# Two small edits in a graph network on one core: the row scaling with one VectorE operation fewer, and a split of rows issued earlier in the first pass

## The chip, the core and the metric

The kernel runs on one core of one Trainium2 chip. The metric is the device time of one execution, in microseconds (us). The engines are called PE (TensorE, matmuls), PEld (its weight loads), DVE (VectorE), ACT (ScalarE), POOL (GpSimd) and SP (SyncE, which here only issues DMAs). Each engine takes its instructions in the order written, and waits where an input or a buffer isn't ready.

## The reference, cut to what matters

Two layers are computed on 16 graphs of 1024 nodes and 128 channels. The first is a gated graph network (four rounds, with a layer norm), which takes up the first 1290 us and isn't touched. The second thins out each adjacency matrix (`adj_d`) and runs three SAGE passes over it, each with a batch norm; then comes a linear head and a layer norm.

```python
def _sage(x, adj, Wr, Wx, b, mf):
    deg = jnp.clip(jnp.sum(adj, axis=-1, keepdims=True), 1.0, None)
    agg = jnp.einsum('bij,bjd->bid', adj, x) / deg
    out = agg @ Wr + x @ Wx + b
    nrm = jnp.maximum(jnp.linalg.norm(out, axis=-1, keepdims=True), NORM_EPS)   # NORM_EPS = 1e-12
    return out / nrm * mf[..., None]

h1 = _bn(jax.nn.relu(_sage(x,  adj_d, Wr1, Wx1, b1, mf)), g1, be1)
h2 = _bn(jax.nn.relu(_sage(h1, adj_d, Wr2, Wx2, b2, mf)), g2, be2)
h3 = _bn(jax.nn.relu(_sage(h2, adj_d, Wr3, Wx3, b3, mf)), g3, be3)
```

The change is in the last line of `_sage`: each row is divided by its norm, which is kept from below 1e-12, and multiplied by the node's mask.

## The kernel before, in words

After the gated layer and the thinning, the class `Sage` runs the passes one after the other. A graph's 1024 rows lie in 8 tiles of 128 partitions, and are worked on in two halves of 4 tiles (512 rows), `f` = 0 and 1. In every pass and for every half, the steps from the matmul results to the finished rows are these:

- `scale_rows` (L1409 to L1419): the aggregated rows times the reciprocal degree (L1417 on DVE; in the third pass L1415 on ACT), plus the second matmul result (L1418 on DVE), gives `s_o`.
- `squares` (L1421 to L1427) on ACT: four sums of squares and a square root give `s_ss`, the norms, one for each row: 128 partitions x 4. The third pass shares them between ACT and DVE (`shared_squares`, L1429).
- `rows` (L1444 to L1452) on DVE: maximum with 1e-12 (L1446), reciprocal (L1447), times the mask (L1448), all on 128x4; then the rows with relu, times these factors (L1451), give `s_r`. In the third pass `rows_by_pool` (L1454) does the same three small operations on DVE (L1456 to L1458), and POOL does the scaling (L1461). There are 66 calls of `rows` (32 each in passes one and two, 2 in pass three) and 30 of `rows_by_pool`.

The first two passes also aggregate the new rows over the adjacency matrix for the pass after. For that the rows are kept as a high and a low part in the matmul's rounded type: `split` (L1464) copies them to `p_rh` on ACT (L1466), and POOL subtracts to get `p_rl` (L1467). `p_at` is the thinned adjacency matrix, transposed.

**The first pass** is a loop over units, one for each graph b, with 16 slots each (`slot`, L1657). No scheduler reorders anything: all engines are under a manual schedule, and the order in `slot` is that of each engine's queue. While graph b is aggregated and its rows are finished, the matrix of graph n = b + 1 is made ready in the same slots:

- `unit` (L1529): four matmuls turn a part of the removal pattern into `p_u`, then ACT writes part of the mask `p_at` from it (L1542). `p_u` has two buffers. In slot 8 ACT writes the whole of it, 128x512.
- `unit_low` (L1545): DVE writes the rest of the mask (L1550). In slot 8 there is none.
- `pack` (L1553): POOL casts the `p_at` of the slot before to bytes (`p_b`, L1558). In slot 8 it packs that of slot 7. SP stores the finished half in slot 10 (L1755).

For graph b, in this order: slots 0, 1, 3, 4 aggregate x (L1618); slots 5 and 7 do `out_first` for the two halves (L1627: `p_oa` and `p_ob`); slots 6 and 8 `scale_rows` and, later in the slot, `squares`; slots 7 and 9 `rows` for half 0 and half 1; slots 8 and 10 `split_r` for half 0 and half 1; slots 11 and 13 transpose the rows (L1472). Slots 9, 10, 12, 14 are the second product (L1618 again): 8 matmuls each, with `p_rh` of half 0, `p_rl` of half 0, `p_rh` of half 1, `p_rl` of half 1. Slots 7 and 12 also split the next graph's x into `p_xh` and `p_xl` on ACT and POOL, and in some slots DVE tests an input tile (L2107).

So the order in slot 8 is: the mask step of the next graph (`unit`), the packing (`pack`), `scale_rows` of half 1, `split_r` of half 0, `squares` of half 1, and a transposition of the next x.

**The second pass** (`slot_second`, L1852) has 8 slots for a graph and the same `rows` in slots 2 and 4. **The third** (`third`, L1917) goes through 32 halves with a distance of two between `scale_rows` and `rows_by_pool`, and ends in the head (`last`).

Of the kernel before, what the change touches and what calls it, by code (L numbers as in the profile page):

```python
# [15 lines left out]
ALU = mybir.AluOpType  # L16
# [349 lines left out]
class Norm:  # L366
# [5 lines left out]
    def __call__(self, out, rows):  # L372
        nc = self.nc
        st = self.pool.tile([P, NB, 6], F32, name="ln_st")
        mv = self.pool.tile([P, NB, 2], F32, name="ln_mv")
        for k in range(NB):
            nc.vector.bn_stats(st[:, k, :], rows[:, k, :])
        for k in range(NB):
            nc.vector.bn_aggr(mv[:, k, :], st[:, k, :])
        rs = self.pool.tile([P, NB], F32, name="ln_rs")  # L380
        nc.scalar.activation(rs, mv[:, :, 1], AF.Sqrt, bias=self.eps)
        nc.vector.reciprocal(rs, rs)
        for k in range(NB):
            nc.vector.tensor_scalar(out[:, k, :], rows[:, k, :], mv[:, k, 0:1], rs[:, k:k + 1],
                                    op0=ALU.subtract, op1=ALU.mult)


def sage_layers(ctx, tc, cst, adj, mask, not_r, summed, x1, W, vec, Wl, bl, out):
# [37 lines left out]
    def transposed(src, n, evac):  # L426
# [6 lines left out]
        return dst  # L433

    def sage(l, b, rows, ht, at, rd, mf, stats, psa, pso):

        pa = [psa.tile([C, HF], F32, name=f"s_a{f}") for f in range(2)]
# [57 lines left out]
    with ExitStack() as c1:  # L495
# [7 lines left out]
        for b in range(B):  # L503
# [36 lines left out]
            for f in range(2):  # L540
                nc.sync.dma_start(adj_t[b][4 * f:4 * f + 4].rearrange("k p n -> p k n"), at4[f])
            mf = row_tile("s_mf", mask[b])
            sage(0, b, rows, ht, at, rd, mf, stats, psa, pso)
        affine = batch_norm(0, stats)

# [85 lines left out]
class FixPoint:  # L631
# [206 lines left out]
    class Block:  # L838
# [22 lines left out]
        def rows(self, g):  # L861
            fix, nc = self.fix, self.fix.nc
            w = fix.wide.tile([P, N], BF, name="f_w", bufs=2)
            nc.vector.tensor_scalar(w, self.us[g], self.q[:, 2, g:g + 1], 0.5, op0=ALU.not_equal, op1=ALU.subtract)
            nr = fix.wide.tile([P, N], BF, name="f_nr", bufs=5)
            nc.vector.tensor_mul(nr, w, self.a[g])
            nc.sync.dma_start(fix.not_r[self.b0 + g, self.k * P:(self.k + 1) * P, :], nr)
            fix.read_last(self.i, g, nr)
# [49 lines left out]
class Gated:  # L918
# [25 lines left out]
    def bank(self):  # L944
        return self.ps6.tile([P, HF], F32, name="h_g")
# [264 lines left out]
class Sage:  # L1210
# [232 lines left out]

    def rows(self, b, f, o, ss):  # L1444
        nc = self.nc
        nc.vector.tensor_scalar(ss, ss, 1e-12, None, op0=ALU.max)  # L1446
        nc.vector.reciprocal(ss, ss)  # L1447
        nc.vector.tensor_mul(ss, ss, self.cst["mask"][:, 4 * f:4 * f + 4, b])  # L1448
        r = self.wk.tile([P, 4, C], F32, name="s_r")
        sc = ss.rearrange("p (k o) -> p k o", o=1).to_broadcast([P, 4, C])  # L1450
        nc.vector.scalar_tensor_tensor(r, o, 0.0, sc, op0=ALU.max, op1=ALU.mult)  # L1451
        return r  # L1452

    def rows_by_pool(self, b, f, o, ss):  # L1454
        nc = self.nc
        nc.vector.tensor_scalar(ss, ss, 1e-12, None, op0=ALU.max)  # L1456
        nc.vector.reciprocal(ss, ss)
        nc.vector.tensor_mul(ss, ss, self.cst["mask"][:, 4 * f:4 * f + 4, b])  # L1458
        r = self.wk.tile([P, 4, C], F32, name="s_r")
        for i in range(4):  # L1460
            nc.gpsimd.tensor_scalar(r[:, i, :], o[:, i, :], ss[:, i:i + 1], 0.0, op0=ALU.mult, op1=ALU.max)  # L1461
        return r
# [194 lines left out]
    def slot(self, b, t):  # L1657

        nc, g, n = self.nc, self.g.get(b), b + 1
        now, nxt = b >= 0, n < B  # L1660

        if nxt:
            if t in (4, 6):
                self.load_nr(n + 1, (t - 4) // 2)
            if t == 7:
                self.load_s(n + 1)
            if t == 10:
                self.load_a(n, 2)
            if t == 13 and n == B - 1:
                self.load_a(n, 3)  # L1670
        loads = {2: 3, 5: 4, 8: 5}
        if b == 0:
            loads = {0: 6, 1: 7, **loads}
        if b == B - 1:
            loads = {0: 4, 2: 5, 4: 7}
        if now and t in loads:
            self.load_a(b, loads[t])

        if now:
            if t in (2, 5):  # L1680
                g["ag", t // 5] = self.evict(g.pop(("pa", t // 5)), -1, 0)
            if t == 15:
                g["ag2"] = [self.evict(g.pop(("pb", f)), b, f) for f in range(2)]
        if nxt:
            self.unit(n, t)
            if t != 6 or not now:
                self.unit_low(n, t)
            if t:
                self.pack(n, t - 1)
        if now and t == 0:  # L1690
            self.pack(b, 15)
        if now:
            bank = lambda: self.ps3.tile([C, HF], F32, name="p_ag")
            if t in (2, 5):
                self.degrees(b, t // 5)
            if t in (0, 1, 3, 4):
                f, lo = t // 3, t in (1, 4)
                if not lo:
                    g["pa", f] = bank()
                self.agg(g["pa", f], (self.xh, self.xl)[lo], g["at"], f, range(NB), not lo, lo)  # L1700
            if t in (5, 7):
                self.out_first(b, t // 7)
            if t in (6, 8):
                f = t // 8
                g["o", f] = self.scale_rows(b, f, g.pop(("oa", f)), g.pop(("ob", f)))
                if t == 6 and nxt:
                    self.unit_low(n, t)
            if t in (3, 6):
                pt = bank() if t == 6 else self.ps1.tile([P, 4, P], F32, name="s_tr").rearrange("p a b -> p (a b)")
                self.degree_columns(b, t // 6, pt[:, :4])  # L1710
            if t in (7, 9):
                f = t // 9
                g["r", f] = self.rows(b, f, g.pop(("o", f)), g.pop(("ss", f)))
            if t in (8, 10):
                self.split_r(b, t // 10)
            if t in (6, 8):
                g["ss", t // 8] = self.squares(g["o", t // 8])
            if t in (11, 13):
                self.turn_r(0, b, t // 13, self.ps1)
            if t in (9, 10, 12, 14):  # L1720
                part = g["rl"] if t in (10, 14) else g["rh"]
                js = range(4 * (t // 12), 4 * (t // 12) + 4)
                for f in range(2):
                    if t == 9:
                        g["pb", f] = bank()
                    self.agg(g["pb", f], part, g["at"], f, js, t == 9, t == 14)

        if nxt:
            if t < 2:
                self.norm_stats(n, t)  # L1730
            if t in (2, 3):
                self.norm(n, t - 2)
            if t in (6, 8):
                self.turn_x(n, t // 8)
            if t in (7, 12):
                self.split_x(n, t // 12)
        tests = {2: 2, 10: 3, 12: 4, 14: 5}
        if b == 0:
            tests = {5: 6, 8: 7, **tests}
        if b == B - 1:  # L1740
            tests = {2: 2, 4: 3, 6: 4, 8: 5, 10: 7}
        if now and t in tests:
            self.check(b, tests[t])

        if now:
            if t == 2:
                nc.sync.dma_start(self.at8[b, 1], g["b", 1])
            if t == 7:
                for i in range(3):
                    nc.sync.dma_start(self.rho[b, i:i + 1, :], g["rho"])  # L1750
            if t in (13, 15):
                nc.sync.dma_start(self.rt[b, t // 15], g["rt", t // 15])
        if nxt:
            if t == 10:
                nc.sync.dma_start(self.at8[n, 0], self.g[n]["b", 0])  # L1755
            if t == 13:
                nc.sync.dma_start(self.x1[n], self.g[n]["s"])
        if (b, t) == (-1, 11):
            self.load_given()
        if (b, t) == (-1, 15):  # L1760

            for i in range(3):
                nc.sync.dma_start(self.rho[:, 3 + i, :], self.mask48[:B, :])
        if (b, t) == (0, 3):
            self.first_weights()
        if t == 1 and b >= 1:
            for f in range(2):
                nc.sync.dma_start(self.ag[b - 1, f], self.g[b - 1]["ag2"][f])
            del self.g[b - 1]
# [426 lines left out]
```

## Time and profile before

| | |
|---|---|
| median of 3 runs | 2141.18 us (2138.12 to 2145.97) |
| the profiled execution | 2138.47 us, its span 2136.5 us |
| PE busy | 2052.7 us, 96% of the span |
| DVE, POOL, ACT busy | 1814.3 (85%), 1333.8 (62%), 1305.9 (61%) |
| first pass, graph by graph | about 1291 to 1713 us of the span, 25.92 us for a unit in the middle |
| second pass | about 1714 to 1958 us |
| third pass | about 1958 to 2066 us, then the head |

In the rows of the profile, `out<-in` are the names of the tiles, and the two numbers ahead of an instruction in the timeline are its start and its duration in us. What stands in square brackets is the time for which the engine was idle before it, and what released it. Ends of matmuls are modelled, as they overlap.

### The profile page before, as it was taken

How to read it: one execution, taken by the hardware profiler on the slowest of the kernel's cores; microseconds unless marked ns; L12 is line 12 of the kernel's file. 1: busy time of each engine (PE TensorE's matmuls, PEld its weight loads, DVE VectorE, ACT ScalarE, POOL GpSimd, SP SyncE). 2: the span in 40 equal slices, each digit the busy share in tenths (PEclk: the TensorE clock that was granted, in tenths of full speed). 3: DMA queues.
4: the chain of work that ended last, by engine and by line, in shares of the span. 5: the costliest groups of instructions: out<-in, count | busy, mean ns of one | idle time of the engine just before them, and what ended most of it. 6: DMA issues, size and time to landing. Idle time of an engine off the chain costs nothing. (4 is left out here: it accounts for less than half of the span.)

```text
span 2136.5 us, 33076 instructions
## 1 busy us (share of the span) xinstructions
PE 2052.7 (96%) x10219; PEld 1435.3 (67%) x10219; DVE 1814.3 (85%) x4194; ACT 1305.9 (61%) x3127; POOL 1333.8 (62%) x1451
## 2 busy tenths in 40 slices
PE   7999999999999999999999988999999989999987
PEld 4566556665566666556665646888888768888876
DVE  4898998988998889998889997888888778887887
ACT  3657557566566565665656656666666545555756
POOL 5458558557467467566476446766677545665866
PEclk9999999999999999999999998999999999999999
DMA  8348346348436357456276346777777489996515
GB/s 252 88 105 252 88 128 224 79 119 240 103 102 222 88 168 188 93 167 184 69 212 159 89 147 245 287 289 286 288 290 285 170 294 341 339 336 222 157 45 161
DMA packets 233855, 406.15 MB, mean 190 GB/s; under 512 B 79042, under 2 KB 100196, under 8 KB 233668
## 3 DMA queue, kind: packets, MB, share of 16 engines
q1 hardware_dynamic: 189348, 284.64, 40.2%
q0 software_dynamic: 41616, 117.98, 20.6%
q8 instruction: 83, 1.36, 0.3%
q10 hardware_dynamic: 2704, 1.31, 0.2%
q14 instruction: 104, 0.85, 0.1%
HBM read 313.48 MB, written 109.25 MB: 198 GB/s over the span
## 5 line engine op out<-in xcount | busy, mean ns | idle before, releaser
L1104 PE MATMUL h_g<-h_h,h_wh 128*128 128x512 f32 x768 | 396.2, 597 | 4.0 <-DVE h_r L1116 4.0
L1104 PE MATMUL h_g<-h_ms,h_wi 128*128 128x512 f32 x768 | 392.2, 592 | 0.0
L1123 POOL TENSOR_TENSOR h_zh<-h_r,h_h 128x512 f32<-128x512 f32 x126 | 174.7, 1387 | 256.4 <-ACT h_r L1119 253.1
L737 DVE TENSOR_TENSOR_SCAN f_rank<-f_a,f_first,f_pd 128x1024 f16<-128x1024 bf16 x128 | 299.4, 2345 | 4.2
L1092 PE MATMUL h_g<-h_a,h_hi 128*128 128x512 f32 x1024 | 278.7, 413 | 1.1 <-DMA h_a<-in_adj_dram 1.0
L1104 PEld LDWEIGHTS h_g<-h_ms,h_wi 128*128 128x128 f32 x768 | 145.5, 190 | 184.3 <-issue 167.9
L1092 PE MATMUL h_g<-h_a,h_lo 128*128 128x512 f32 x1024 | 261.8, 392 | 0.1
L1558 POOL CAST p_b<-p_at 128x512 uint8<-128x512 f32 x256 | 203.7, 817 | 86.9 <-DVE p_at L1550 48.5
L1092 PEld LDWEIGHTS h_g<-h_a,h_hi 128*128 128x128 f32 x1024 | 190.1, 188 | 61.9 <-issue 20.8
L1092 PEld LDWEIGHTS h_g<-h_a,h_lo 128*128 128x128 f32 x1024 | 189.8, 188 | 38.7 <-DVE h_lo L1030 0.6
L1104 PEld LDWEIGHTS h_g<-h_h,h_wh 128*128 128x128 f32 x768 | 133.3, 190 | 101.2 <-issue 72.6
L1125 POOL TENSOR_TENSOR h_h<-h_h,h_zh 128x512 f32<-128x512 f32 x126 | 179.8, 1427 | 9.9
L1119 ACT ACTIVATE h_r<-h_r,h_bi 128x512 f32<-128x512 f32 x128 | 92.4, 722 | 150.7 <-DVE h_r L1118 150.7
L1124 POOL TENSOR_TENSOR h_zh<-h_z,h_zh 128x512 f32<-128x512 f32 x126 | 162.2, 1287 | 9.9
L1095 ACT COPY h_ms<-h_g 128x512 f32<-128x512 f32 x128 | 73.8, 577 | 150.0 <-PE h_g L1092 149.7
L1425 ACT ACTIVATE s_junk<-s_o 128x128 bf16<-128x128 f32 x256 | 76.1, 298 | 130.3 <-DVE s_o L1418 130.3
L910 ACT ACTIVATE f_u<-f_rank,f_q 128x128 f16<-128x128 f16 (+7 forms) x128 | 110.5, 866 | 70.6 <-DVE f_rank L850 69.6
L2107 DVE SCALAR_TENSOR_TENSOR p_a<-p_a 128x1024 bf16<-128x1024 f32 x96 | 126.3, 1315 | 0.0
L778 POOL TENSOR_SCALAR_AFFINE_SELECT f_both<-f_both 128x512 bf16<-128x512 bf16 x32 | 20.6, 642 | 163.9 <-DVE f_both L777 163.9
L1838 PE MATMUL q_ob<-s_wxp,q_xt 128*128 128x256 f32 x512 | 122.3, 382 | 0.0
L887 ACT ACTIVATE f_pd<-f_rank,f_q 128x128 f32<-128x128 f16 x128 | 59.1, 462 | 98.0 <-DVE f_q L701 94.8
L1550 DVE SCALAR_TENSOR_TENSOR p_at<-p_nr,p_u 128x128 fp32r<-128x128 bf16 (+1 forms) x192 | 102.6, 541 | 16.5 <-ACT p_at L1542 10.0
(306 smaller groups left out, 4895.8 us busy)
## 6 DMA issues: line engine op xcount, KB each, us to landing
h_a<-in_adj_dram POOLq DMA_DIRECT2D x128, 512.0 KB, 9.3
p_a<-in_adj_dram SPq DMA_DIRECT2D x96, 512.0 KB
f_a<-in_adj_dram POOLq DMA_DIRECT2D x128, 256.0 KB, 6.4
e_nr<-f_nr SPq DMA_DIRECT2D x128, 256.0 KB
p_nr<-e_nr SPq DMA_DIRECT2D x32, 1024.0 KB
s_at<-p_b SPq DMA_DIRECT2D x32, 512.0 KB
s_ag<-s_ag SPq DMA_DIRECT2D x64, 256.0 KB
q_agi<-s_ag SPq DMA_DIRECT2D x32, 512.0 KB
```

The costliest lines, as they stand in the source:

```text
L737: nc.vector.tensor_tensor_scan(out, a, other[:, 0, 0:1].to_broadcast([P, N]), start, op0=ALU.add, op1=ALU.bypass)
L910: nc.scalar.activation(u[:, :n1], rank[:, g, :n1], AF.Abs, bias=q[:, 1, g:g + 1], scale=q[:, 0, g:g + 1])
L1092: nc.tensor.matmul(pm[f], part[:, j, :], st.adj[j][:, half[f]], start=(j == 0 and n == 0), stop=(j == NB - 1 and n == 1))
L1104: nc.tensor.matmul(pg, lhs, rhs, start=(i == 0), stop=(i == len(mm) - 1))
L1119: nc.scalar.activation(r, r, AF.Tanh, bias=bias(self.bi, 2))
L1123: aid.tensor_tensor(d, r, h, ALU.subtract)
L1124: aid.tensor_tensor(d, z, d, ALU.mult)
L1125: aid.tensor_tensor(h, h, d, ALU.add)
L1550: self.nc.vector.scalar_tensor_tensor(g["at"][:, j, c0:c0 + low], v[:, j, c0:c0 + low], 0.0, pu[:, :low], op0=ALU.is_lt, op1=ALU.is_lt)
L1558: self.nc.gpsimd.tensor_copy(g["b", f][:, j, :], g["at"][:, j, f * HF:(f + 1) * HF].bitcast(F32))
L1838: nc.tensor.matmul(pb[:, i], g["xt"][:, f, blk], self.wxp, start=(i % 2 == 0), stop=False)
L2107: nc.vector.scalar_tensor_tensor(junk, a, 0.0, a, op0=ALU.is_gt, op1=ALU.not_equal, accum_out=bad[:, c:c + 1])
```

## The change

In `rows` and `rows_by_pool` the maximum ahead of the reciprocal is taken out. The reciprocal is taken of the norm itself, and the mask's multiplication becomes one operation that first takes the minimum with 1e12. In `slot`, `split_r` of half 0 moves from behind `scale_rows` in slot 8 to ahead of `unit` and `pack`. `split_r` of half 1 in slot 10 stays.

```diff
     def rows(self, b, f, o, ss):
         nc = self.nc
-        nc.vector.tensor_scalar(ss, ss, 1e-12, None, op0=ALU.max)
         nc.vector.reciprocal(ss, ss)
-        nc.vector.tensor_mul(ss, ss, self.cst["mask"][:, 4 * f:4 * f + 4, b])
+        nc.vector.scalar_tensor_tensor(ss, ss, 1e12, self.cst["mask"][:, 4 * f:4 * f + 4, b],
+                                       op0=ALU.min, op1=ALU.mult)
         r = self.wk.tile([P, 4, C], F32, name="s_r")
...
     def rows_by_pool(self, b, f, o, ss):
         nc = self.nc
-        nc.vector.tensor_scalar(ss, ss, 1e-12, None, op0=ALU.max)
         nc.vector.reciprocal(ss, ss)
-        nc.vector.tensor_mul(ss, ss, self.cst["mask"][:, 4 * f:4 * f + 4, b])
+        nc.vector.scalar_tensor_tensor(ss, ss, 1e12, self.cst["mask"][:, 4 * f:4 * f + 4, b],
+                                       op0=ALU.min, op1=ALU.mult)
...
     def slot(self, b, t):
...
             if t == 15:
                 g["ag2"] = [self.evict(g.pop(("pb", f)), b, f) for f in range(2)]
+            if t == 8:
+                self.split_r(b, 0)
         if nxt:
             self.unit(n, t)
...
-            if t in (8, 10):
-                self.split_r(b, t // 10)
+            if t == 10:
+                self.split_r(b, 1)
```

## The prediction

> **What bounds the kernel now.** I read the page first, for the engine that has no slack, then PE's waits, then a table by stage, and last the order in time of one unit of the first pass, where the moved step lies.
>
> ```profile
> span 2136.5 us, 33076 instructions
> ...
> PE 2052.7 (96%) x10219; PEld 1435.3 (67%) x10219; DVE 1814.3 (85%) x4194; ACT 1305.9 (61%) x3127; POOL 1333.8 (62%) x1451
> ...
> PE 33%; DVE 3%; ACT 2%; POOL 1%; issue 1%; DMA 0%; DVEq 0%; ACTq 0%; POOLq 0%
> ```
>
> PE is busy 96% of the span and has far the largest share of the chain that ended last. A shorter DVE step is worth something only where PE, or that chain, stands waiting for it. So the next view is PE's waits over the whole span; columns are total us, times, longest.
>
> ```profile
> PE p_ag L1618 <- ACT p_rh L1466: 10.2, 16, 2.2
> ...
> PE s_tr L1472 <- DVE s_r L1451: 3.3, 3, 1.7
> ...
> PE p_ag L1618 <- POOL p_rl L1467: 0.9, 1, 0.9
> ```
>
> The first is the largest of all of PE's waits: once in each of the 16 units of pass one, PE stands until ScalarE has written the high part `p_rh` of the first half's rows. The timeline gives 0.64 us to unit 0 and 2.20 to unit 15 (which has no next unit beside it), so 10.2 - 0.64 - 2.20 = 7.4 is left for 14 units, 0.52 each. The table by stage, over 13 of these:
>
> ```profile
> core 0: us, PE busy (x) PEld busy (x) DVE busy (x) ACT busy (x) POOL busy (x), PEclk, DMA share, GB/s
> 1341.50:1679.00 337.50, 330.16 (x2498) 271.76 (x2497) 281.67 (x756) 233.32 (x664) 236.96 (x261) 1.00 0.77 279
> ```
>
> 337.5 - 330.2 = 7.3 us of PE idle: nearly all of it is this wait. A unit lasts 25.92 us (the second product starts at 1419.81 and again at 1445.74). No other engine is over 84% here. Now the last steps before the wait, in one unit:
>
> ```profile
> 1417.33 0.20 ACT L1426 ACTIVATE s_ss<-s_ss 128x4 f32<-128x4 f32 x1
> ...
> 1417.57 0.17 DVE L1446 TENSOR_SCALAR s_ss<-s_ss 128x4 f32<-128x4 f32 x1
> 1417.78 0.18 DVE L1447 RECIPROCAL s_ss<-s_ss 128x4 f32<-128x4 f32 x1
> ...
> 1417.99 0.17 DVE L1448 TENSOR_TENSOR s_ss<-s_ss,mask 128x4 f32<-128x4 f32 x1
> ...
> 1418.26 0.69 DVE L1451 SCALAR_TENSOR_TENSOR s_r<-s_o,s_ss 128x512 f32<-128x512 f32 x1
> ...
> 1418.66 0.60 ACT L1542 ACTIVATE p_at<-p_u 128x512 fp32r<-128x512 f32 x1
> ...
> 1418.90 0.39 PE L1537 MATMUL p_u<-ident_b,p_nr 128*128 128x128 bf16 x4
> 1419.15 0.61 ACT L1466 CAST p_rh<-s_r 128x512 fp32r<-128x512 f32 x1
> ...
> 1419.81 2.11 PE L1618 MATMUL p_ag<-p_at,p_rh 128*128 128x512 f32 x8 [0.52 <-ACT p_rh L1466]
> ```
>
> The rows `s_r` are done at 1418.95, but `p_rh` starts at 1419.15: ScalarE's mask step of slot 8 (L1542) came first. PE's own work is done at 1419.29 and it starts 0.52 later. The same unit goes on, with the second half of the rows:
>
> ```profile
> 1420.60 1.29 POOL L1467 TENSOR_TENSOR p_rl<-s_r,p_rh 128x512 fp32r<-128x512 f32 x1
> ...
> 1421.84 0.60 POOL L1558 CAST p_b<-p_at 128x512 uint8<-128x512 f32 x1
> 1421.93 0.54 DVE L1446 TENSOR_SCALAR s_ss<-s_ss 128x4 f32<-128x4 f32 x1 [1.59 <-ACT s_ss L1426]
> ...
> 1421.97 2.09 PE L1618 MATMUL p_ag<-p_at,p_rl 128*128 128x512 f32 x8
> ...
> 1424.13 0.62 ACT L1466 CAST p_rh<-s_r 128x512 fp32r<-128x512 f32 x1 [0.77 <-DVE s_r L1451]
> ...
> 1424.80 2.12 PE L1618 MATMUL p_ag<-p_at,p_rh 128*128 128x512 f32 x8
> ```
>
> Two deadlines lie right behind the wait: the low part `p_rl` ends at 1421.89 and PE wants it at 1421.97; the second half's `p_rh` ends at 1424.75 and PE starts on it at 1424.80. Neither shows as a wait, neither has slack. If PE comes earlier, they must come earlier too.
>
> **What the Trainium skill says.** "VectorE: DVE Perf Modes", section "Rules for kernel authors": on DVE the number of operations counts. The trace agrees for four elements a row: 147 to 178 ns of busy time, 200 to 210 ns from start to start. "SBUF — State Buffer", section "Who interferes with whom": a DVE operation with two SBUF inputs can't run beside a GpSimd one that reads SBUF, nor can a `tensor_scalar` in a two-port mode; the later waits for the whole of the earlier. The trace agrees: L1446 lasts 169 ns in the median, but 540 above, until POOL's cast ended at 1422.44, and 929 at worst; L1451 goes from 694 to 1752.
>
> **Part 1, one DVE operation fewer (96 calls).** Out go a TENSOR_SCALAR (0.15 to 0.17 us) and a TENSOR_TENSOR (0.165), in comes one SCALAR_TENSOR_TENSOR on 128x4. The trace has it on 128x8 (L1581, 0.17 us); I take 0.17. Bounds: 0.15, and 0.93 when POOL holds the port (L1446's worst). Net: one start-to-start step, 0.20 us less from `s_ss` to `s_r`. Where it counts:
> - First pass, first half: it is on the chain to PE's wait. Second half: 0.20 us inherited, because DVE takes up the second half's scaling (L1417, L1418) right behind `s_r`, and 0.20 of its own or more, as the operation that goes is the one POOL held up.
> - Second pass: nothing in the steady part. PE is busy 213.7 of 217 us between 1728 and 1945, and that hides it. At its start (1726 to 1731) the chain runs through L1446 twice and PE waits for `s_r`: 2 x 0.20 = 0.4 us. The blocked L1451 at 1731.32 (1.75 us, behind POOL's low part) could give more (0.9) if DVE now gets there first, or only 0.2.
> - Third pass: PE is the bound (96.7 of 98 us). One dip (1975 to 1990) has L1456 on the chain: 0.2 us (0 to 0.5). At the end the last two `rows` stand in DVE's queue on the chain (2061.91 and 2063.89): 2 x 0.20 = 0.4.
>
> **Part 2, the split of half 0 moved up.** It issues two instructions and no DMA: ScalarE's copy to `p_rh` (0.61), now ahead of the mask step L1542 of slot 8, and POOL's subtraction to `p_rl` (1.29), now ahead of the packing of slot 7 (0.60). ScalarE: `p_rh` follows `s_r` at once, 1418.95 - 0.20 = 1418.75, start 1418.80 instead of 1419.15. Gain **0.35 us**, of which 0.20 is part 1 and 0.15 the order. PE would start at 1419.46; its own work ends at 1419.29, so 0.17 us of the wait is left. Behind `p_rh` now queues L1542, done about 1419.9 instead of 1419.26; its readers are the packing of slot 8 and, by its buffer, the mask matmuls of slot 10 (1421.77), and the squares behind it begin at 1420.2: covered. POOL: `p_rl` starts when the low part of x ends (1420.0) instead of behind a packing (1420.60), and ends at about 1421.3. PE wants it at 1421.97 - 0.35 = 1421.62. Without this the gain would be lost here, as 1421.89 is too late. The packing of slot 7 ends at 1421.9 instead of 1420.63; SP's store of the packed half waits for it (issued 1420.65, now about 1421.9), and behind it SP has nothing until 1425.75: no cost.
> Second half: `s_ss` 1421.50 to 1421.70, reciprocal 1421.73, the new operation 1421.94 but held by a packing to about 1422.4, `s_r` 1422.67 to 1423.36 (1423.9 if held too), `p_rh` done at 1424.0 (1424.6). PE wants it at 1424.80 - 0.05 - 0.35 = 1424.40. It fits, or costs 0.2.
>
> **Sum.** Units 1 to 14: 14 x 0.35 = 4.9. Unit 0: 0.2 at `p_rh`, then PE's 0.9 us wait for `p_rl`, of which 0.1 to 0.9 goes (POOL and the input test L2107 start within 0.1 us of each other there): 0.6. Unit 15: no masks to pass, 0.2. Start of the second pass 0.4, dip 0.2, end 0.4. Together **6.7 us**. The profiled execution took 2138.47 (span 2136.5 and 2.0 around it), so 2131.8; the median of the three runs is 2.7 above it, and from that 2141.2 - 6.7 = **2134.5 us**.
>
> **Rivals.**
> - *The wait goes wholly, and the locks fall well* (0.20): 7.4 in units 1 to 14, 1.1 in unit 0, 0.2, 0.9, 0.5 and 0.4: 10.5, so 2130.7. For it: the 0.17 us left rests on modelled matmul ends. Against: the chain has only 0.35 to give.
> - *The wait moves to slot 12* (0.14): the second `p_rh` comes only at 1424.6, PE loses 0.2 again, 14 x 0.15 + 1.8 = 3.9, so 2137.3. For it: zero slack before. Against: that half gains 0.4 by itself.
> - *Slower: POOL's shifted packings hold the second half's DVE steps* (0.08). Three casts and `p_rl` now run nearly without a gap from 1420.0 to 1422.5, where the new two-input operation and `s_r` fall. With the worst durations seen (0.93 and 1.75), `s_r` ends at 1424.7 and PE starts at 1425.4, 0.6 later than now: 14 x 0.6 = 8.4, less the other 1.8: +6.6, so 2147.8. It decides against the change once `s_r` of the second half ends later than it did, 1424.1. Against: POOL is free after 1422.5 until the next `p_rh`.
> - *The change doesn't do what it says*: where the new operation is as slow as the two it replaces, only the order counts, 14 x 0.15: inside the second rival's range.
>
> **Chances.** The main case has 0.58. A measurement tells about 0.5% from no change, 10.7 us. Faster by more: about 0.6 of the first rival and 0.08 of the main case (run-to-run spread here is 8 us), 0.17. Slower by more: some half of the slower rival and a rest for the unseen, 0.06. Within: 0.77. The range reaches from gains of 12.5 to a loss of 2.3: 2128.7 to 2143.5.
>
> **What will show it.** Right: DVE has 96 instructions fewer; the wait of L1618 for `p_rh` falls from 0.52 to about 0.17 in a unit and its total to some 5 us; a unit lasts 25.57; `p_rh` of half 0 stands ahead of slot 8's L1542, `p_rl` ahead of the packing. Wrong: a new wait of PE for `p_rl` in slot 10 or `p_rh` in slot 12, L1451 longer in the second half, or a unit that stays at 25.92.

## The result, and the profile after

The median went from 2141.83 us (7 runs) to **2131.95 us** (7 runs): a ratio of **0.9963, with a 95% interval of 0.9952 to 0.9974**, that is 7.9 us less (5.6 to 10.3). The ratio on record isn't the quotient of the two medians: these lie 9.9 us apart (0.9954), which is inside the interval too. A second measurement of the changed kernel on another occasion gave 0.9964 (0.9951 to 0.9977). The profiled execution took 2132.37 us. Its page begins:

```profile
span 2130.4 us, 32979 instructions
...
PE 2052.9 (96%) x10218; PEld 1437.5 (67%) x10219; DVE 1784.6 (84%) x4098; ACT 1304.9 (61%) x3127; POOL 1339.8 (63%) x1451
```

DVE has 4194 - 4098 = 96 operations fewer; PE is as busy as it was, so what went is waiting. PE's waits in the changed kernel (us, times, longest):

```profile
PE p_ag L1618 <- ACT p_rh L1466: 5.5, 16, 2.0
...
PE q_ag L1878 <- POOL q_at L1829: 3.4, 2, 1.9
...
PE s_tr L1472 <- DVE s_r L1451: 1.1, 2, 0.7
```

The wait that the change aims at fell from 10.2 to 5.5 us. In the second pass the wait for `s_r` fell too, but one for POOL's unpacking (`q_at`) stands in its place, once at the start of the pass (1.86 us) and once at its end (1.56). And the same unit of the first pass as the prediction shows, in the timeline of the changed kernel:

```profile
1416.90 0.17 DVE L1447 SCALAR_TENSOR_TENSOR s_ss<-s_ss,mask 128x4 f32<-128x4 f32 x1
...
1417.17 0.69 DVE L1451 SCALAR_TENSOR_TENSOR s_r<-s_o,s_ss 128x512 f32<-128x512 f32 x1
...
1417.95 0.62 ACT L1466 CAST p_rh<-s_r 128x512 fp32r<-128x512 f32 x1 [0.30 <-DVE s_r L1451]
...
1418.47 0.59 ACT L1542 ACTIVATE p_at<-p_u 128x512 fp32r<-128x512 f32 x1
...
1418.62 2.12 PE L1618 MATMUL p_ag<-p_at,p_rh 128*128 128x512 f32 x8 [0.22 <-ACT p_rh L1466]
1418.95 1.31 POOL L1467 TENSOR_TENSOR p_rl<-s_r,p_rh 128x512 fp32r<-128x512 f32 x1
...
1420.79 2.09 PE L1618 MATMUL p_ag<-p_at,p_rl 128*128 128x512 f32 x8
...
1420.84 0.18 DVE L1446 RECIPROCAL s_ss<-s_ss 128x4 f32<-128x4 f32 x1 [1.58 <-ACT s_ss L1426]
1421.05 0.33 DVE L1447 SCALAR_TENSOR_TENSOR s_ss<-s_ss,mask 128x4 f32<-128x4 f32 x1
...
1422.21 0.62 ACT L1466 CAST p_rh<-s_r 128x512 fp32r<-128x512 f32 x1
```

The copy to `p_rh` now goes ahead of the mask step, and ScalarE waits 0.30 us for `s_r` where before it was busy. PE's wait is 0.22 instead of 0.52. `p_rl` is done at 1420.26, half a microsecond ahead of PE (1420.79); the second half's `p_rh` at 1422.83, 0.76 ahead of PE (1423.59).

Where the time went, from the starts of PE's matmuls in the two traces (us):

| stretch | before | after | difference |
|---|---|---|---|
| start to the first aggregation of unit 0 (not touched) | 1293.1 | 1294.4 | +1.3 |
| from there to the second product of unit 1 | 48.9 | 47.5 | -1.4 |
| 13 units more | 337.0 | 332.5 | -4.4 |
| from unit 14's second product to the first matmul of pass two (`q_oa`) | 39.9 | 37.9 | -2.0 |
| pass two: to the second graph's first matmul | 19.5 | 21.0 | +1.6 |
| rest of pass two | 215.0 | 215.1 | +0.1 |
| pass three, to the head's bank start (L1405) | 118.4 | 116.6 | -1.8 |
| head | 64.8 | 65.3 | +0.6 |

A unit lasts (1674.39 - 1341.88)/13 = 25.58 us instead of 25.92. Only the row of the 13 units is as steady as that: in the two traces of the changed kernel a unit agrees within 0.01 us. Other rows also move where nothing was edited. In the second trace of the changed kernel (k8), for instance, the second row is 46.0 and not 47.5 us, and with the first pass as before (k6) it is 50.3 and not 48.9. Over all traces the start took 1291.2 to 1294.4 us and the head 64.8 to 66.7, in no order that follows the edits. The experiments show what of the other rows belongs to the change.

### The profile page after: what moved, and what is told of

It reads as the page before. It is cut to its first block, busy times and chain, and to the rows that moved or that the text cites. A ratio compares the mean times of both kernels' runs of the same rounds, so it can differ in the third digit from the quotient of the medians.

```text
span 2130.4 us, 32979 instructions
## 1 busy us (share of the span) xinstructions
PE 2052.9 (96%) x10218; PEld 1437.5 (67%) x10219; DVE 1784.6 (84%) x4098; ACT 1304.9 (61%) x3127; POOL 1339.8 (63%) x1451
```

## Experiments

Each has a short name (k1 to k9), by which later sections refer to it. Ratios are to the kernel before. A diff is against the changed kernel unless the text says otherwise.

**Each part alone.** First part 1 without the move (k1):

```diff
-            if t == 8:
-                self.split_r(b, 0)
...
-            if t == 10:
-                self.split_r(b, 1)
+            if t in (8, 10):
+                self.split_r(b, t // 10)
```

> Part 1 alone: the DVE operation fewer in rows and rows_by_pool, the split of half 0 left behind the mask step and the packing. Theory (two gates): in units 1 to 14 the copy to p_rh waits for whichever comes last, s_r or ScalarE's mask step, and that step can't begin before PE's p_u of slot 8; the copy would start 0.49 us behind it as before. So the unit stays at 25.92 us and the wait at 0.52, though s_r is 0.20 us earlier; what is left is unit 15 and the third pass, 0.5 to 2 us of the whole. Rival (the two parts add up, 0.20 and 0.15, as the prediction's sum had it): the unit is 25.72, the wait 0.32, and the whole 3.5 to 5 us shorter than before.

Ratio to before 0.9991 (0.9983 to 1.0000). A unit lasts (1680.87 - 1344.34)/13 = 25.89 us, PE waits 0.52. Its timeline in a unit:

```profile
1368.46 0.69 DVE L1451 SCALAR_TENSOR_TENSOR s_r<-s_o,s_ss 128x512 f32<-128x512 f32 x1
1369.07 0.60 ACT L1542 ACTIVATE p_at<-p_u 128x512 fp32r<-128x512 f32 x1
1369.56 0.61 ACT L1466 CAST p_rh<-s_r 128x512 fp32r<-128x512 f32 x1
1370.22 0.76 PEld L1618 LDWEIGHTS p_ag<-p_at,p_rh 128*128 128x128 f32 x4 [0.70 <-ACT p_rh L1466]
```

`s_r` is there at 1369.15, yet the copy starts at 1369.56, 0.49 behind the mask step, as it did before. The two-gate theory holds.

Then part 2 alone (k2), with the three small operations as they were, in `rows` (shown) and in `rows_by_pool`:

```diff
+        nc.vector.tensor_scalar(ss, ss, 1e-12, None, op0=ALU.max)
         nc.vector.reciprocal(ss, ss)
-        nc.vector.scalar_tensor_tensor(ss, ss, 1e12, self.cst["mask"][:, 4 * f:4 * f + 4, b],
-                                       op0=ALU.min, op1=ALU.mult)
+        nc.vector.tensor_mul(ss, ss, self.cst["mask"][:, 4 * f:4 * f + 4, b])
```

> Part 2 alone: the split of half 0 moved up, the three small operations kept. Theory (two gates, and no slack behind them): p_rh of half 0 comes 0.15 us earlier, the wait in slot 9 falls to about 0.37, but the second half's rows come no earlier than before, so PE finds p_rh of half 1 missing in slot 12 and waits 0.1 there: the unit is 25.85 to 25.92, the whole 0 to 1.5 us shorter. Rival (the parts add up): the unit is 25.77, no wait in slot 12, the whole about 2 to 3 us shorter.

Ratio 0.9996 (0.9988 to 1.0004); a unit lasts (1677.95 - 1341.00)/13 = 25.92 us. In its timeline the wait in slot 9 is shorter by 0.10, and slot 12 takes it back:

```profile
1366.92 2.11 PE L1618 MATMUL p_ag<-p_at,p_rh 128*128 128x512 f32 x8 [0.42 <-ACT p_rh L1466]
...
1369.08 2.09 PE L1618 MATMUL p_ag<-p_at,p_rl 128*128 128x512 f32 x8
...
1371.34 0.62 ACT L1466 CAST p_rh<-s_r 128x512 fp32r<-128x512 f32 x1 [0.77 <-DVE s_r L1451]
...
1372.01 1.65 PE L1618 MATMUL p_ag<-p_at,p_rh 128*128 128x512 f32 x6
```

From the low part's product to the second half's, PE takes 1372.01 - 1369.08 = 2.93 us, where the kernel before takes 2.83 (1421.97 to 1424.80) and the changed one 2.80 (1420.79 to 1423.59). The copy ends at 1371.96 and PE starts 0.05 later: a new wait, though the trace marks none. So the parts bring 0.03 and 0.00 us to a unit alone, and 0.34 together.

**The second half's own saving.** The changed kernel, with the old three operations in slot 9 alone (k5; the new argument `three` of `rows` asks for them):

```diff
-                g["r", f] = self.rows(b, f, g.pop(("o", f)), g.pop(("ss", f)))
+                g["r", f] = self.rows(b, f, g.pop(("o", f)), g.pop(("ss", f)), three=(f == 1))
```

> The changed kernel, with the old three small operations in the first pass's half 1 (slot 9) alone. Theory (the second deadline needs that half's own saving): half 1 then inherits 0.20 us but not its own, and the TENSOR_SCALAR is held by POOL's packings again; p_rh of half 1 ends at about PE's demand or 0.1 to 0.2 later, PE waits in slot 12, and the unit is 25.68 to 25.78 instead of 25.58; the whole 1.4 to 2.8 us above the changed kernel. Rival (inheriting is enough): the unit stays at 25.58, no wait in slot 12.

Ratio 0.9970 (0.9962 to 0.9978), a unit of (1675.03 - 1340.66)/13 = 25.72 us: 0.14 of the 0.34 is gone. In its timeline (L1447 is the maximum, L1456 the rows, L1471 the copy in this kernel):

```profile
1342.88 0.53 DVE L1447 TENSOR_SCALAR s_ss<-s_ss 128x4 f32<-128x4 f32 x1 [1.59 <-ACT s_ss L1426]
...
1343.93 1.11 DVE L1456 SCALAR_TENSOR_TENSOR s_r<-s_o,s_ss 128x512 f32<-128x512 f32 x1
...
1345.08 0.62 ACT L1471 CAST p_rh<-s_r 128x512 fp32r<-128x512 f32 x1 [0.76 <-DVE s_r L1456]
```

The maximum lasts 0.53 us beside POOL's casts, and the rows 1.11. From reading the norms to the copy it takes 1345.08 - 1342.88 = 2.20 us; in the changed kernel 1422.21 - 1420.84 = 1.37. Inheriting 0.20 us wasn't enough: PE again takes 2.93 us from the low part's product to the second half's, as in k2. With the operation fewer neither is held so long, 0.33 and 0.69 us in the unit shown above.

**POOL's order.** The changed kernel with the copy moved up, but the subtraction back behind the packing (k3):

```diff
             if t == 8:
-                self.split_r(b, 0)
+                g["rh"] = self.wk.tile([P, NB, C], FR, name="p_rh", bufs=1)
+                g["rl"] = self.wk.tile([P, NB, C], FR, name="p_rl", bufs=1)
+                nc.scalar.copy(g["rh"][:, :4, :], g["r", 0])
...
+            if t == 8:
+                self.nc.gpsimd.tensor_tensor(g["rl"][:, :4, :], g["r", 0], g["rh"][:, :4, :].bitcast(F32),
+                                             ALU.subtract)
```

> The changed kernel, but of the split of half 0 only ScalarE's copy is moved up; POOL's subtraction stays behind the packing of slot 7 as before. Theory: p_rl then ends 0.6 us later than in the changed kernel, where it was done 0.5 us ahead of PE; PE waits for it in slot 10 for 0.1 to 0.2 us, the unit is 25.7 to 25.75, the whole about 2 us longer than the changed kernel. Rival (POOL's order doesn't matter, what counts is the copy): the unit stays at 25.58.

Ratio 0.9966 (0.9954 to 0.9978), which can't be told from the changed kernel's. The trace can: a unit lasts (1672.84 - 1339.09)/13 = 25.67 us, 0.09 more, a little less than expected.

```profile
1391.31 1.29 POOL L1719 TENSOR_TENSOR p_rl<-s_r,p_rh 128x512 fp32r<-128x512 f32 x1
...
1392.66 1.66 PE L1618 MATMUL p_ag<-p_at,p_rl 128*128 128x512 f32 x6
```

`p_rl` ends at 1392.60 and PE starts right behind it, 2.23 us after the high part's product (1390.43) instead of 2.17. In unit 0 the order on POOL counts for more. There PE waits for `p_rl` for 0.94 us, as it did before (0.86) and in k1 (0.71); in every kernel with the subtraction moved up that wait is gone, though in k2 and k5 0.4 to 0.5 us of it come back in slot 12.

**What is left of the wait.** The changed kernel with the copy of half 0 in two instructions of two tiles (k4):

```diff
-        self.nc.scalar.copy(hi[to], src[:, :, c0:])
+        w = 4 // parts
+        for i in range(parts):
+            k = 4 * f + w * i
+            self.nc.scalar.copy(hi[:, k:k + w, c0:], src[:, w * i:w * (i + 1), c0:])
...
-                self.split_r(b, 0)
+                self.split_r(b, 0, 2)
```

> The changed kernel, with ScalarE's copy of half 0 to p_rh in two instructions of two tiles each. Theory: what is left of PE's wait (0.22 us) ends with the first of them, which takes about 0.38 instead of 0.61; the second ends 0.1 later than the whole copy did, and PE gets to its tiles 0.48 later: the wait goes to 0 to 0.03, the unit to 25.36 to 25.40, the whole 2.5 to 3.3 us below the changed kernel. Rival (the rest of the wait is PE's own time, hidden by the modelled ends of its matmuls, or PE waits for the copy of all four tiles): the unit stays at 25.5 to 25.58.

Ratio 0.9947 (0.9934 to 0.9961). A unit lasts (1670.67 - 1340.89)/13 = 25.37 us, and PE is busy 337.4 of 337.5 us in the table by stage.

```profile
1391.16 0.71 ACT L1469 CAST p_rh<-s_r 128x256 fp32r<-128x256 f32 x2 [0.30 <-DVE s_r L1451]
1391.62 1.70 PEld L1621 LDWEIGHTS p_ag<-p_at,p_rh 128*128 128x128 f32 x8 [0.18 <-ACT p_rh L1469]
```

PE loads its first weights 0.46 us after the first copy began, and not 0.67. The wait was real, not a matter of modelled ends. The two copies together take ScalarE 0.71 us instead of 0.62. Both kernels once more, on one chip (k8 the changed kernel, k9 that with two copies):

> The changed kernel itself, once more, beside the version with two copies on one chip. Theory: a ratio to before of 0.996 to 0.997 again; a unit of 25.58 us; at the start of the second pass PE waits about 1.9 us for POOL's unpacking, and the loss of a further 1.3 us in the first profile (granted clock 0.50 for some 3 us) doesn't come back, so that from the first transposition of rows to the next graph's first matmul it takes 10.5 us as in the other kernels with the operation fewer. Rival (the lower clock belongs to the changed kernel's order): 11.8 us again.

> The version with two copies, once more, beside the changed kernel on one chip. Theory: 2.5 to 3.5 us below the changed kernel (a ratio to before of 0.9945 to 0.9955), a unit of 25.37 us with no wait of PE in slot 9. Rival (what the units gain is given back at the starts of the later passes): within 1 us of the changed kernel.

The changed kernel 2130.24 us, 0.9964 (0.9951 to 0.9977), unit 25.58; with two copies 2127.48 us, 0.9949 (0.9937 to 0.9961), unit 25.37. The intervals overlap, so the whole alone doesn't settle it. But the medians are 2.8 us apart, and 14 units that are shorter by 0.21 us give 2.9: this version beats the changed kernel too.

**The third pass.** The kernel before, with the operation fewer in the third pass alone (k6; the diff is against the kernel before):

```diff
     def rows_by_pool(self, b, f, o, ss):
         nc = self.nc
-        nc.vector.tensor_scalar(ss, ss, 1e-12, None, op0=ALU.max)
         nc.vector.reciprocal(ss, ss)
-        nc.vector.tensor_mul(ss, ss, self.cst["mask"][:, 4 * f:4 * f + 4, b])
+        nc.vector.scalar_tensor_tensor(ss, ss, 1e12, self.cst["mask"][:, 4 * f:4 * f + 4, b],
+                                       op0=ALU.min, op1=ALU.mult)
...
-                    rows = self.rows_by_pool if i < len(units) else self.rows
+                    rows = self.rows_by_pool if i < len(units) else (lambda *a: self.rows(*a, three=False))
```

> The kernel before, with the operation fewer in the third pass alone (first and second pass and the order in slot 8 as before). Theory (the third pass's ring of POOL, ACT and DVE through three buffers is about as long as PE's three halves, so 0.2 us less in it takes away most of the stalls after the ring has once been late): the third pass, from its first matmul to the head's last start of a bank, lasts about 116.6 us instead of 118.4, and the whole is 1.7 us shorter than before. Rival (the pieces of the prediction: 0.2 in the dip and 0.4 at the end, the rest chance): 117.8, the whole 0.6 us shorter. The first pass stays at 25.92 for a unit, and the start of the second keeps its waits for s_r, 2.6 us together.

Ratio 0.9993 (0.9986 to 1.0000), 1.5 us (0 to 3.0). The pass lasts 2072.61 - 1956.17 = 116.4 us, the first pass's unit 25.92. Over all traces the pass took 118.4 (before) and 118.2 (part 2 alone) with the old operations; without, 116.4 to 116.6 in five and 117.5, 117.7 and 118.3 in three. (A ninth, 119.8, began at a low clock, see below.) The traces say where the difference lies. From the pass's first matmul to that of its last half it takes 103.2 and 103.3 us with the old operations and 102.4 to 102.5 in all eight without; of these 0.7 to 0.8 us, 0.2 to 0.4 come from PE's one long wait in the middle (1.32 us before). The rest is the tail behind the last half, where PE waits for POOL's scaled rows (L1461). Before and in the changed kernel:

```profile
PE s_tr L1472 <- POOL s_r L1461: 2.1, 4, 1.1
...
PE s_tr L1472 <- POOL s_r L1461: 0.7, 2, 0.4
```

That wait is 2.1 us in both traces with the old operations, 0.7 in the five short ones without, and 2.1 to 2.3 in the other three, k8 with the changed kernel itself among them. So 0.7 to 0.8 us belong to the removed operation. The further 1.0 us comes and goes with one and the same kernel; as only two traces have the old operations, it stays open whether they can have the short tail too.

**The start of the second pass.** Before, and then in the changed kernel's first profile:

```profile
1731.26 1.27 POOL L1467 TENSOR_TENSOR q_rl<-s_r,q_rh 128x512 fp32r<-128x512 f32 x1 [13.67 <-DMA q_b<-s_at]
1731.32 1.75 DVE L1451 SCALAR_TENSOR_TENSOR s_r<-s_o,s_ss 128x512 f32<-128x512 f32 x1
```

```profile
1724.86 0.69 DVE L1451 SCALAR_TENSOR_TENSOR s_r<-s_o,s_ss 128x512 f32<-128x512 f32 x1
1725.00 1.68 POOL L1467 TENSOR_TENSOR q_rl<-s_r,q_rh 128x512 fp32r<-128x512 f32 x1 [13.91 <-ACT q_rh L1466]
...
1726.62 1.50 POOL L1829 CAST q_at<-q_b 128x1024 fp32r<-128x1024 uint8 x1
...
1728.18 1.22 PE L1878 MATMUL q_ag<-q_at,q_rh 128*128 128x512 f32 x2 [1.86 <-POOL q_at L1829]
```

Before, POOL's low part of half 0 started 0.06 us ahead of the rows `s_r` of half 1, and these were held (1.75 us). Now the rows start first and the low part is held (1.68 instead of 1.27), and PE waits for the cast behind it. In all kernels with the operation fewer that pass through here in this order, PE's wait for `s_r` is 0.9 to 1.1 us and that for the cast 1.9; in those without it, 2.6 and 0.4. From the first transposition of rows to the second graph's first matmul it takes 10.53 to 10.56 us in the three traces with the old operations here (before, k2, k6), 10.47 to 10.51 in six without (k8 among them), and 11.8 only in this one, where the table by stage shows a granted clock of 0.50 between 1728 and 1731. That 1.3 us didn't come back. In the last experiment (k7), k4 once more, POOL also unpacks two pieces first:

```diff
+                if b == 0:
+                    self.unpack(b, 0)
+                    self.unpack(b, 2)
                 self.split(0, g["r", 0], g["rh"], g["rl"])
...
-            if b < B:
+            if b < B and (b or t not in (3, 5)):
```

> The changed kernel with the copy of half 0 in two instructions, and at the start of the second pass POOL unpacks its first two pieces of the matrix ahead of the first graph's low part instead of behind it. Theory: at that start PE waits for POOL's unpacking (1.9 us) only because the low part stands ahead of it in POOL's queue while POOL was idle for over 10 us; from the first transposition of rows to the next graph's first matmul it takes about 9.3 us instead of 10.5, that wait goes or falls under 0.7, and the whole is 1.2 us below the kernel with the two copies alone. Rival (the bytes to unpack arrive no earlier than that): 10.5 us as before, or more, since the low part then waits too.

The stretch lasts 1729.03 - 1720.71 = 8.3 us and the wait for the cast is gone there: the bytes had been in place. The whole doesn't show it: 0.9945 (0.9926 to 0.9963), against 0.9947; a gain of 1.2 us can't be seen inside intervals of 3 us and more to each side. In its trace a wait of 0.5 us for POOL comes back one graph later, the rest of the pass takes 215.9 us instead of 215.1, and pass three starts at a low clock (0.50 between 1946 and 1948; its first group of matmuls took 1.96 us, not 1.13). Whether that is chance or belongs to the edit stays open.

## Why the prediction was right, and where it wasn't

Its total, 6.7 us, lies within the measured 5.6 to 10.3, and the 2134.5 us forecast are 2.5 above the measured median. By its own steps:

- **The wait in slot 9**: right. 0.35 us a unit was forecast, 0.34 measured; 0.17 was to be left, 0.22 is. So 0.31 of the gain is the wait itself; the other 0.03 lies between the products of slots 10, 12 and 14, where the trace marks no wait (k1 gains just these 0.03). Slots 10 and 12 fit, as worked out, and neither the slower rival nor that of a wait moving to slot 12 came: the new operation took 0.357 us at worst (L1447), not 0.93 (one call in each of k1, k3 and k7 took 0.79 to 0.90). `s_r` of the second half, which POOL had held to 1.11 us in the kernel before, took 0.69, so slot 12 had 0.76 us of slack where 0.4 had been forecast.
- **"0.20 is part 1 and 0.15 the order"**: wrong, though the sum of the two is right, as it was read off as one move of the copy, from 1419.15 to 1418.80. The copy had two gates, `s_r` and the mask step, and the next product a third in slot 12. Alone, the parts bring 0.03 and 0.00 (k1, k2). The last rival, where only the order counts, would have brought 14 x 0.00 and not 14 x 0.15.
- **"Without this the gain would be lost here"**, of POOL's subtraction: too strong for units 1 to 14, where 0.09 of 0.34 is lost (k3); the second half's own operation holds more, 0.14 (k5). It is true of unit 0.
- **Unit 0**: mis-sized within its range. 0.6 was forecast, 0.2 at `p_rh` and the rest at `p_rl`, of whose 0.86 us 0.1 to 0.9 was to go. The wait for `p_rh` fell from 0.64 to 0.43, and from unit 0's second product to unit 1's it takes 25.74 us instead of 26.99 (25.74 again in k8, 26.88 in k6); less unit 1's own 0.34 that is 0.9, so 1.1 together. POOL got ahead of the input test (`p_rl` at 1316.59, the test at 1316.74), so the 0.86 us wait went whole. Which of the two would start first was open, and the forecast took the middle.
- **Unit 15**: 0.2, as its wait went from 2.20 to 1.99. The other 1.8 us of that row of the table don't belong to the change: the same stretch took 38.4 to 41.4 us in the experiments, in no order that follows the edits (40.1 in k8).
- **Start of the second pass**: mis-sized. 0.4 was forecast. The first of its two 0.20 came (3.94 to 3.73 us from the second half's `q_oa` to the transposition); of the second there came 0.06 (10.53 to 10.56 against 10.47 to 10.51). The prediction saw that DVE might get the port first and counted that as a gain of up to 0.9; POOL's cast was next in line, and PE waits for both.
- **Third pass**: mis-sized. The dip was priced at 0.2 (0 to 0.5), as one operation on the chain; 0.7 to 0.8 came, since smaller stalls went with it. For the end 0.4 was forecast; in five traces the tail is 1.0 us shorter than before and in three it isn't.

Added up from the traces, the steps give 14 x 0.34 = 4.8, then 1.1, 0.2, 0.3 and 0.7 to 1.8, together 7.1 to 8.2 us, where 7.9 was measured. The forecast of 6.7 is low by unit 0 and the third pass. That it fell inside an interval 4.7 us wide doesn't prove these smaller steps.

## What to carry to other kernels

When an instruction waits on two things that end close together, price them as a maximum and not as a sum: take away each alone before saying which one paid. Behind a wait that is to go, look for the next deadlines without slack; the trace shows no wait there until the first one is gone. If a consumer starts with a part of a tile, let the producer write that part first: it was worth more than half as much as the whole change in the middle of the first pass (0.21 against 0.34 us a unit).

## What the hardware showed beyond that

- The port that DVE and POOL share (the Trainium skill, "SBUF — State Buffer", section "Who interferes with whom": issue order decides who blocks) changed hands for a whole pass, and the traces agree on what decides: 0.06 us ahead, POOL held DVE for 1.75 us; 0.14 us behind, it was held itself. In the second pass before, 16 of the 32 calls of L1451 were held (up to 1.75 us); after, all 32 took 0.69. It is the same in all three traces with the old operations here and in all eight without. DVE's busy time between 1728 and 1945 fell from 185.6 to 166.7 us, more than the removed operations' 0.165 us each explain, and POOL's low part takes up to 1.83 us instead of 1.30. So 0.2 us on one engine turned the order. PE, busy there, gained nothing (215.0 and 215.1 us), and at the last graph of the pass it again waits for POOL's cast (1.56 us) where it had waited for `s_r` and the cast (0.70 and 0.43).
- Once, after a wait of PE of 1.86 us, the granted clock was 0.50 for some 3 us, and the stretch took 1.3 us longer. In six other traces the same wait came without that. What decided it isn't shown.
